# Joining the two layers of a two-layer attention network: layer 1's weights, first image and first projections move beside layer 0's last image, and the fallback branch moves to the program's end

## The chip, the cores and the metric

The kernel runs on one core of a Trainium2 chip. The metric is the device time of one execution in microseconds. All arithmetic is in 32-bit floats, except the feed-forward's weights, which hold signs.

## The reference

The input x has 8 images of 384 channels and 32 x 32 positions. Layer 0 is group norm (32 groups), an attention of 8 heads of 48 channels with a bias that depends on the relative position (from a small MLP), an output projection and the residual:

```python
qkv = (tokens @ qkv_w + qkv_b).reshape(b, n, 3, NUM_HEADS, HEAD_DIM)
attn = jnp.einsum('bhnd,bhmd->bhnm', q * scale, k) + relative_bias
attn = jax.nn.softmax(attn, axis=-1)
x = x + (attn_times_v @ proj_w + proj_b)
```

Layer 1 works on the 1024 tokens of each image: layer norm, an attention of 6 heads of 64 channels whose q and k are normalised over the 64 channels of a head, the residual, layer norm again, and a feed-forward of two linear maps with binarised weights (sign of the weight less its group's mean), whose outputs are scaled by the largest absolute value of a group of images. The groups are five of one image each, so images 5, 6 and 7 have a feed-forward that is zero.

```python
q, k = _normalize(q), _normalize(k)          # (t - mean) / std over a head's 64 channels
t = t + softmax(q @ k.T * scale) @ v @ proj_w.T + proj_b
h = gelu(quantize(ln(t) @ sign(W1 - mean).T + b1))
t = t + quantize(h @ sign(W2 - mean).T + b2)
```

## The kernel before

Two functions follow each other, `_layer0` (L97) and `_layer1` (L892); layer 0's result goes through a tensor x1 in DRAM. Each layer has pools of its own in SBUF and four PSUM tiles of two banks. Each engine runs its instructions in the order of the program text, since both layers are traced under a manual schedule; only the range check between them is ordered by a scheduler. `_Later` (L64) holds work that is due a number of steps later; `later.step()` runs once per unit or projection, and so writes the order of the engines' queues by hand. A "unit" is a pair of heads, a half of the queries and a quarter of the keys.

Layer 0: per image 32 units. `scores` (L419) makes 16 matmul instructions into two PSUM tiles s, DVE adds the position bias into an e tile (L437), ACT takes the exponential (L441); `weigh` (L447) multiplies e by v two units later (`LAG`). No row maximum is subtracted. The row sums come out as a row of the product; when a pair of heads is done, `divide` (L474) sends them through DRAM to 128 partitions, POOL takes the power -1 (L486), and after some steps the inverses come back spread over the rows (L494) and POOL multiplies (L498). The image's output projection, `project_out` (L514), normally runs at unit 3 of the next image. The last image has no next: it multiplies the first three pairs, calls `later.finish()`, and then multiplies the last pair, `wl`, into the same three PSUM tiles (L526), adds the residual (L538) and stores x1 (L541).

Since no maximum is subtracted, all row sums are kept in `sums`, and a range check (L593 to L603) reduces them to one flag. Its maximum over the partitions is a custom instruction of POOL (L602). The program loads the flag into registers and branches over `_layer0_shifted`, a slower general layer 0 that redoes x1, before `_layer1` begins:

```python
    _layer0(tc, ins, x1, flag)
    out_of_range = tc.nc.values_load(flag[0:1, 0:1])
    with tc.If(out_of_range > 0):
        _layer0_shifted(tc, ins, x1)
    _layer1(tc, ins, x1, out)
```

The flag is zero for the given inputs.

Layer 1 begins with the loads of its weights `L1_attn_qkv_wT` (L922) and its first image `bx` (L917). `center` (L957) subtracts from the projection's weights their mean over the input channels (18 matmul instructions with a matrix of ones, named cm, a copy on ACT, subtractions on DVE at L973) and their mean over a head's channels (L977 to L979), so that the layer norm's and the head's means need no work later. `attention_inputs` (L1458) then makes the token sums (squares on ACT, `token_sums`, named ts, tr, td, tc), the six projections of q and k (pq, L1023), head sums (hs, L1052), and `normalise_qk` (L1060): the sums go to DRAM (hd), to 128 partitions (hc), POOL takes a power (L1073), the result goes to DRAM (hi), the factors of k come back as kc, and those of q, spread over the rows, as rq (L1087); DVE multiplies q by rq (L1094). Its two step numbers say after how many steps rq is fetched and after how many more it is used. Last come the projections of v (pv, L1104). `sign_weights` (L1121) loads the feed-forward's weights in five raw tiles each, DVE sums them (L1139), a matmul gives the means (L1143), ACT writes the signs (L1147); a table in the main loop gives the step of each. All intermediate tiles of 128 x 1024 come from one pool of 16, `work`.

Attention in layer 1 has 24 units per image; ACT reads the scores from PSUM and applies kc as its scale (L1179). In images 0 to 4 the feed-forward is mixed with the next image's projections; images 6 and 7 get theirs from `attention_inputs`, as image 0 does.

## Time and profile before

| | |
|---|---|
| median of three runs | 3165.62 us (3164.66 to 3168.25) |
| the profiled execution's own time | 3169.41 us |
| its span, first to last instruction | 3166.5 us |
| mean granted TensorE clock | 0.988 |
| PE, DVE, ACT, POOL busy | 97%, 55%, 44%, 14% |
| layer 0's last output products begin | 1442.04 us |
| SP's first DMA of layer 1 | 1478.50 us |
| first scores of layer 1 | 1569.16 us |

PE is the matmul engine, PEld its weight loads, DVE, ACT, POOL and SP the vector, scalar, GpSimd and sync engines. A line of the timeline has the start and length in us, the engine, the line of the program, the operation, what it writes and reads, how many instructions it groups, and in brackets how long the engine had been idle and what ended that; "<-issue" means that the profile shows nothing it waited for. A matmul of 32-bit floats in the text is two instructions in the profile.

### The profile page before, as it was taken

The page shows a single profiled execution, that of the slowest core. Times are in us where ns is not written, and L with a number is a line of the kernel's source. Part 1 is how long each engine was busy: PE and PEld are TensorE (multiplying, and loading weights), DVE is VectorE, ACT ScalarE, POOL GpSimd, SP SyncE. Part 2 cuts the span into 40 slices and gives each one's busy share as a digit, 9 for nine tenths or more (in the row PEclk, how much of TensorE's full clock was granted, in tenths as well). Part 3 has the DMA queues.
Part 4 walks back from the last instruction along what each step waited for, and adds up shares of the span by engine and source line. Part 5 has one row for each costly group of instructions (what it writes and reads, how often), then busy time and mean ns, then how long its engine had stood idle before and what let it go on. Part 6 is the DMA issues. An engine that isn't in the chain of part 4 may idle for free.

```text
span 3166.5 us, 46012 instructions
## 1 busy us (share of the span) xinstructions
PE 3057.7 (97%) x19066; PEld 1572.0 (50%) x19066; DVE 1744.7 (55%) x1748; ACT 1400.7 (44%) x1763; POOL 458.8 (14%) x302
## 2 busy tenths in 40 slices
PE   8799999999999999996899999999999999999999
PEld 3254645455555546432445645645645555634343
DVE  2554737373645647273464764754754854844545
ACT  2452616252543526162272462553553643643535
POOL 0110202111111102021200301301201201211110
PEclk9899999999999999998999999999999999999999
DMA  7302020211212020203310110100101101101011
GB/s 178 107 18 79 22 82 16 69 35 25 73 23 81 19 79 22 62 16 105 75 42 22 44 33 22 62 17 21 61 22 27 51 22 29 53 18 62 15 49 42
DMA packets 102768, 150.49 MB, mean 48 GB/s; under 512 B 62260, under 2 KB 65828, under 8 KB 101784
## 3 DMA queue, kind: packets, MB, share of 16 engines
q1 hardware_dynamic: 99688, 147.41, 16.5%
q8 instruction: 153, 2.51, 0.3%
q14 instruction: 63, 0.52, 0.1%
q10 hardware_dynamic: 2864, 0.05, 0.1%
HBM read 111.05 MB, written 27.32 MB: 44 GB/s over the span
## 4 chain that ended last, share of the span: by engine, by line
PE 42%; DVE 4%; DMA 3%; ACT 2%; issue 1%; POOL 1%; SPq 0%; DVEq 0%; ACTq 0%; POOLq 0%
PE s L1168 11%; PE o L1217 10%; PE y2p L1419 5%; PE pq L1023 5%; PE pp L1279 4%; PE y1p L1365 3%; PE pv L1104 3%; POOL hc L1073 1%; PE sum L1240 1%; DVE lun L1319 1%; DVE un L1314 1%; DVE un L1311 1%; DMA rb<-rd 1%; PE tsa L992 1%; PE hs L1052 0%
## 5 line engine op out<-in xcount | busy, mean ns | idle before, releaser
L441 ACT ACTIVATE e<-e 128x1024 f32<-128x1024 f32 x512 | 534.8, 1056 | 461.6 <-DVE e L437 445.6
L437 DVE TENSOR_TENSOR e<-s,grow 128x1024 f32<-128x1024 f32 x512 | 601.1, 1218 | 190.6 <-PE s L426 186.9
L426 PE MATMUL s<-qk 48*64 48x512 f32 x4096 | 613.8, 595 | 23.3 <-DVE e L437 20.3
L457 PE MATMUL o<-e,v 64*64 64x512 f32 x4096 | 608.5, 592 | 0.0
L1179 ACT ACTIVATE e<-s,kc 128x512 f32<-128x512 f32 x768 | 463.5, 691 | 213.3 <-PE s L1168 195.3
L1168 PE MATMUL s<-qk,qk 64*64 64x512 f32 x3072 | 400.6, 601 | 9.9 <-DVE v L1114 9.1
L1217 PE MATMUL o<-e,v 64*64 64x512 f32 x3072 | 391.6, 591 | 0.2 <-ACT e L1179 0.2
L426 PEld LDWEIGHTS s<-qk 48*64 48x64 f32 x4096 | 232.3, 133 | 259.4 <-issue 92.8
L457 PEld LDWEIGHTS o<-e,v 64*64 64x64 f32 x4096 | 249.3, 134 | 192.6 <-issue 96.2
L1194 DVE TENSOR_TENSOR t<-t,e 128x1024 f32<-128x1024 f32 x192 | 231.3, 1222 | 79.2 <-ACT e L1179 79.2
L1023 PE MATMUL pq<-bx,L_attn_qkv_wT 128*128 128x512 f32 x576 | 254.4, 596 | 2.3 <-DVE L_attn_qkv_wT L979 2.1
L372 PE MATMUL pq<-xn,wqk 128*128 128x512 f32 x576 | 251.0, 597 | 1.8 <-DVE xn L353 1.8
L1168 PEld LDWEIGHTS s<-qk,qk 64*64 64x64 f32 x3072 | 146.0, 134 | 211.5 <-issue 128.2
L486 POOL TENSOR_TENSOR inv<-sums,over 128x16 f32<-128x16 f32 x32 | 92.9, 2904 | 1033.1 <-DMA sums<-sd 927.1
L1217 PEld LDWEIGHTS o<-e,v 64*64 64x64 f32 x3072 | 138.8, 133 | 191.4 <-issue 164.6
L372 PEld LDWEIGHTS pq<-xn,wqk 128*128 128x128 f32 x576 | 109.4, 191 | 143.6 <-issue 142.9
L1023 PEld LDWEIGHTS pq<-bx,L_attn_qkv_wT 128*128 128x128 f32 x576 | 107.7, 190 | 145.7 <-issue 140.4
L1191 DVE TENSOR_TENSOR t<-e,e 128x1024 f32<-128x1024 f32 x96 | 114.1, 1224 | 84.1 <-ACT e L1179 84.1
L1352 DVE TENSOR_REDUCE parts<-y 128x1 f32<-128x1024 f32 x75 | 90.0, 1218 | 95.2 <-ACT y L1349 95.0
L1073 POOL TENSOR_TENSOR hc<-hc,rsqrt 128x32 f32<-128x32 f32 x24 | 135.3, 5639 | 2.0
L1039 ACT ACTIVATE qsq<-pq 128x1024 f32<-128x1024 f32 x48 | 49.1, 1024 | 192.5 <-DVE qk L1033 92.1
L1104 PE MATMUL pv<-L_attn_qkv_wT,bx 128*128 128x384 f32 x384 | 130.9, 497 | 1.9 <-DVE meanL_ffn_W1T L1144 1.9
(149 smaller groups left out, 2935.3 us busy)
## 6 DMA issues: line engine op xcount, KB each, us to landing
rb<-rd SPq DMA_DIRECT2D x112, 256.0 KB
wide<-table SPq DMA_DIRECT2D x128, 114.2 KB
xn<-in_x_dram SPq DMA_DIRECT2D x24, 512.0 KB
res<-in_x_dram SPq DMA_DIRECT2D x24, 512.0 KB
x<-res SPq DMA_DIRECT2D x24, 512.0 KB
bx<-x SPq DMA_DIRECT2D x8, 1536.0 KB
rq<-hi SPq DMA_DIRECT2D x48, 256.0 KB
out_dram<-bx SPq DMA_DIRECT2D x24, 512.0 KB
```

Source lines behind the costliest of these rows:

```text
L372: nc.tensor.matmul(pq[:, h], wqk[:, k, s, 2 * pair : 2 * pair + 2, :].rearrange("p h d -> p (h d)"), xn[:, k, ts(h, HALF)], start=(k == 0) ...
L426: nc.tensor.matmul(s[j][ts(c, QP), i], qk[pair][rows, 1, ts(4 * m2 + 2 * i + c, QP)], qk[pair][rows, 0, ts(h, HALF)], start=True, stop=True,)
L437: nc.vector.tensor_add(e.rearrange("p (i q) -> p i q", i=2), s[j], bass.AP(near.tensor, near.offset, [near.ap[0], [-QROWS * IW, 2], [1, HA ...
L441: nc.scalar.activation(e, e, AF.Exp)
L457: nc.tensor.matmul(po[ts(j, S0), r], v[keys, 2 * m2 + i, 2 * pair + j, :], es[j][keys, ts(i, HALF)], start=(m2 == 0 and i == 0), stop=(m2 ...
L1023: nc.tensor.matmul(pq[:, h], wqkv[:, k, s * C + pair * P : s * C + (pair + 1) * P], xt[:, k, ts(h, HALF)], start=(k == 0), stop=(k == KC - 1),
L1073: nc.gpsimd.tensor_tensor(c, c, rsqrt.to_broadcast(list(c.shape)), ALU.pow)
L1104: nc.tensor.matmul(pv[:, i, 0:C], xt[:, k].rearrange("c (p m) -> c m p", m=MT)[:, 2 * m2 + i], wqkv[:, k, 2 * C : 3 * C], start=(k == 0), ...
L1168: nc.tensor.matmul(s[j][ts(c, QP), i], qk[pair, 1][rows, ts(4 * m2 + 2 * i + c, QP)], qk[pair, 0][rows, ts(h, HALF)], start=True, stop=True,)
L1179: nc.scalar.activation(e[:, ts(i, HALF)], s[j][:, i], AF.Exp, scale=kc[:, pair, j, m : m + 1])
L1194: nc.vector.tensor_add(total[j], total[j], e)
L1217: nc.tensor.matmul(po[ts(j, D1), r], v[keys, 2 * m2 + i, at : at + D1], es[j][keys, ts(i, HALF)], start=(m2 == 0 and i == 0), stop=(m2 == ...
```

## The change

The branch with the general path goes to the end of the program: if the flag is set, `_layer0_shifted` and then a whole second `_layer1` run and overwrite the output. So layer 1 no longer waits for the flag, and the two layers are traced under one manual schedule. The range check's five DVE and one POOL instructions become five stages that run at steps 5, 7, 9, 11 and 13 of image 1 of layer 1, on tiles of `work`.

Both layers share one PSUM pool, the constants `rsqrt` and `ones`, one place for an image and one for the projection's weights (`_Shared`). Layer 0's q, k and v weights become two views of one tile. In layer 1 even images use the shared place, odd ones a place of their own; before, they alternated between two. `_Start` holds what was the head of layer 1 and is called from units 5 to 23 of layer 0's last image: weights, image, the two halves of centring with ACT's copies into two of layer 0's nine e tiles, the subtractions on POOL instead of DVE.

What layer 0 needs for its last projection (`wp`, `wl`, `oT`, `rb` and others) moves to a pool `kept` on the other side of SBUF that stays open. `project_out` is split: after the last unit come the products of three pairs and `later.finish()`; the residual loads go out when layer 1 has made its first pools; the products of the last pair, the sums and the stores run at step 1 of layer 1, which is after its token sums and its first projection. Layer 1's pools take the option `reuse_waits="tile"`; `wide` and a new pool `room` (for w1, w2, rb) open only after that step. The steps of the raw weights and of the head normalisation in `attention_inputs` change. The main loops are the same but for their indentation.

```diff
+class _Shared:
+    def __init__(self, tc, ctx):
+        nc = tc.nc
+        self.pool = ctx.enter_context(tc.tile_pool(name="s_pool", bufs=1))
+        self.ps = ctx.enter_context(tc.tile_pool(name="s_ps", bufs=4, space=PSUM))
+        self.rsqrt = self.pool.tile([P, 1], F32, tag="rsqrt", name="rsqrt")
+        nc.gpsimd.memset(self.rsqrt, -0.5)
+        self.ones = self.pool.tile([P, P], F32, tag="ones", name="ones")
+        nc.gpsimd.memset(self.ones, 1.0)
+    def mm2(self, name):
+        return self.ps.tile([P, NH, HALF], F32, tag="p", name=name)
+    def image(self, name):
+        return self.pool.tile([P, KC, N], F32, tag="x", name=name)
+    def weights(self, name):
+        return self.pool.tile([P, KC * 3 * C], F32, tag="w", name=name)
+class _Start:
+    def __init__(self, tc, ins, x1, shared):
+        self.nc, self.ins, self.x1, self.shared = tc.nc, ins, x1, shared
+    def load_weights(self):
+        self.wqkv = self.shared.weights("wqkv").rearrange("p (k c) -> p k c", k=KC)
+        self.nc.sync.dma_start(
+            self.wqkv, self.ins["L1_attn_qkv_wT"].rearrange("(k p) c -> p k c", p=P)
+        )
+    def load_image(self):
+        self.image = self.shared.image("bx0")
+        self.nc.sync.dma_start(self.image, self.x1[0].rearrange("(k p) n -> p k n", p=P))
+    def means(self, temp, at, n):
+        nc = self.nc
+        pm = self.shared.mm2(f"cm{at}")
+        for h in range(-(-n // HALF)):
+            w = min(HALF, n - h * HALF)
+            for k in range(KC):
+                cols = slice(at + h * HALF, at + h * HALF + w)
+                nc.tensor.matmul(
+                    pm[:, h, :w], self.shared.ones, self.wqkv[:, k, cols],
+                    start=(k == 0), stop=(k == KC - 1),
+                )
+        self.mean = temp(f"cmean{at}")
+        nc.scalar.activation(
+            self.mean[:, :n], pm.rearrange("p h q -> p (h q)")[:, :n], AF.Copy, scale=1.0 / C
+        )
+    def subtract(self, at, n):
+        for k in range(KC):
+            w = self.wqkv[:, k, at : at + n]
+            self.nc.gpsimd.tensor_sub(w, w, self.mean[:, :n])
+    def heads(self, k):
+        nc = self.nc
+        w = self.wqkv[:, k, 0 : 2 * C].rearrange("p (h d) -> p h d", d=D1)
+        hm = self.shared.pool.tile([P, 2 * H1], F32, tag="hm", name=f"hm{k}")
+        nc.vector.tensor_reduce(hm, w, AX.X, ALU.add)
+        nc.gpsimd.tensor_scalar(hm, hm, 1.0 / D1, 1.0, ALU.mult, ALU.mult)
+        nc.gpsimd.tensor_sub(w, w, hm.unsqueeze(2).to_broadcast([P, 2 * H1, D1]))
+    def stages(self, temp):
+        first, rest = (0, 2 * HALF), (2 * HALF, 3 * C - 2 * HALF)
+        return [
+            (5, self.load_weights),
+            (6, self.load_image),
+            (10, lambda: self.means(temp, *first)),
+            (11, lambda: self.subtract(*first)),
+            (12, lambda: self.means(temp, *rest)),
+            (14, lambda: self.subtract(*rest)),
+            (19, lambda: self.heads(0)),
+            (21, lambda: self.heads(1)),
+            (23, lambda: self.heads(2)),
+        ]
-def _layer0(tc, ins, x1, flag):
+def _layer0(tc, ins, x1, sums, shared, beside):
...
+    keep = ExitStack()
+    kept = keep.enter_context(tc.tile_pool(name="a_kept", bufs=1, side="right"))
...
-        wqk = const.tile([P, KC, 2, 2 * NF0, S0], F32, tag="wqk", name="wqk")
-        wv = const.tile([P, KC, C], F32, tag="wv", name="wv")
+        both = shared.weights("w0")
+        wqk = both[:, 0 : KC * 2 * C].rearrange(
+            "p (k s h d) -> p k s h d", k=KC, s=2, d=S0
+        )
+        wv = both[:, KC * 2 * C :].rearrange("p (k c) -> p k c", k=KC)
...
+        pps = {}
+        def products(b, m, pairs):
+            if (b, m) not in pps:
+                pps[b, m] = mm2(f"pp{b}_{m}")
+            for k in pairs:
+                for h in range(NH):
+                    nc.tensor.matmul(
+                        pps[b, m][:, h], (wp[:, k] if k < NF0 else wl)[:, ts(m, P)],
+                        oT[:, k, ts(h, HALF)],
+                        start=(k == 0), stop=(k == (NF0 if b == B - 1 else NF0 - 1)),
+                    )
+        def residuals(b, temp):
+            res = []
             for m in range(KC):
-                res.append(etile(f"res{b}_{m}"))
+                res.append(temp(f"res{b}_{m}"))
                 nc.sync.dma_start(res[m], x[b, ts(m, P)].rearrange("p h w -> p (h w)"))
-            def products(m, pairs):
-                if pps[m] is None:
-                    pps[m] = mm2(f"pp{b}_{m}")
-                for k in pairs:
-                    for h in range(NH):
-                        nc.tensor.matmul(
-                            pps[m][:, h], (wp[:, k] if k < NF0 else wl)[:, ts(m, P)],
-                            oT[:, k, ts(h, HALF)],
-                            start=(k == 0), stop=(k == (NF0 if apart else NF0 - 1)),
-                        )
-            if apart:
-                for m in range(KC):
-                    products(m, range(NF0))
-                later.finish()
+            return res
+        def project_out(b, res, pairs):
             for m in range(KC):
-                products(m, range(NF0, NP0) if apart else range(NF0))
+                products(b, m, pairs)
                 nc.vector.scalar_tensor_tensor(
-                    res[m], flat2(pps[m]), bp[:, m : m + 1], res[m], ALU.add, ALU.add
+                    res[m], flat2(pps[b, m]), bp[:, m : m + 1], res[m], ALU.add, ALU.add
                 )
                 nc.sync.dma_start(x1[b][ts(m, P), :], res[m])
...
+        with_last = beside(etile)
...
+                if b == B - 1:
+                    for at, work in with_last:
+                        if at == i:
+                            work()
                 later.step()
...
+        for m in range(KC):
+            products(B - 1, m, range(NF0))
+        later.finish()
+    def load_rest(temp):
+        rest.extend(residuals(B - 1, temp))
+    def finish():
+        project_out(B - 1, rest, range(NF0, NP0))
+        keep.close()
+    rest = []
+    return load_rest, finish
...
+def _range_check(tc, sums, flag, temp):
...
+    return [
+        over, under, lambda: nc.vector.tensor_mul(good[0], good[0], every), worst,
+        lambda: nc.vector.tensor_copy(flag, bad[1][:, 0:1]),
+    ]
...
-def _layer1(tc, ins, x1, out):
+def _layer1(tc, ins, x1, out, shared, start, before=None, check=None):
...
+            return ctx.enter_context(tc.tile_pool(name=name, bufs=bufs, reuse_waits="tile"))
...
+            if b % 2 == 0:
+                t = shared.image(f"bx{b}")
+            else:
+                t = xp.tile([P, KC, N], F32, tag="x", name=f"bx{b}")
...
-        wqkv = chunked("L1_attn_qkv_wT", 3 * C)
-        first = load(0)
+        if before is not None:
+            before[0](wtile)
+        wqkv, first = start.wqkv, start.image
...
+        def rest_of_pools():
+            nonlocal wide, room, w1, w2
+            if before is not None:
+                before[1]()
+            wide = pool("b_wide", 1)
+            room = pool("b_room", 1)
+            w1 = room.tile([P, KC, FF], F32R, tag="w1", name="w1")
+            w2 = room.tile([P, FC, C], F32R, tag="w2", name="w2")
...
-                        head(pair - 1, 2, 1)
+                        head(pair - 1, *((3, 3) if pair == 1 else (5, 4)))
...
-            center()
-                ("L1_ffn_W1T", w1, 1, (4, 4, 4, 5, 5), 6, (7, 7, 8, 8, 9)),
-                ("L1_ffn_W2T", w2, 4, (7, 7, 8, 8, 9), 10, (11, 13, 15, 17, 19)),
+            ("L1_ffn_W1T", lambda: w1, (KC, FF // NG), 2, (5, 5, 5, 6, 6), 8, (9, 9, 9, 10, 10)),
+            ("L1_ffn_W2T", lambda: w2, (FC, C // NG), 7, (10, 11, 12, 13, 14), 16, (17, 18, 19, 22, 23)),
...
+        later.after(1, rest_of_pools)
         qk, kc = attention_inputs(0, xt)
...
+            if b == 1 and check is not None:
+                for i, stage in enumerate(check(wtile)):
+                    later.after(2 * i + 5, stage)
...
-    _layer0(tc, ins, x1, flag)
+    sums = state.tile([P, B, NP0, 2 * N // P], F32, tag="sums", name="sums")
+    with ExitStack() as main, tc.manual_schedule():
+        shared = _Shared(tc, main)
+        start = _Start(tc, ins, x1, shared)
+        before = _layer0(tc, ins, x1, sums, shared, start.stages)
+        _layer1(
+            tc, ins, x1, out, shared, start, before,
+            lambda temp: _range_check(tc, sums, flag, lambda name: temp(name, (P, HALF))),
+        )
     out_of_range = tc.nc.values_load(flag[0:1, 0:1])
     with tc.If(out_of_range > 0):
         _layer0_shifted(tc, ins, x1)
-    _layer1(tc, ins, x1, out)
+        with ExitStack() as again, tc.manual_schedule():
+            shared = _Shared(tc, again)
+            start = _Start(tc, ins, x1, shared)
+            late = again.enter_context(tc.tile_pool(name="late", bufs=2))
+            for _, stage in start.stages(
+                lambda name: late.tile([P, N], F32, tag="t", name=name)
+            ):
+                stage()
+            _layer1(tc, ins, x1, out, shared, start)
```

## The prediction

> **What bounds the kernel now.** I read the page first (busy shares, then the forty slices), then a table of busy times by stage over the end of layer 0 and the start of layer 1, then the chain and the timeline there, and last the queue of SP.
>
> ```profile
> PE 3057.7 (97%) x19066; PEld 1572.0 (50%) x19066; DVE 1744.7 (55%) x1748; ACT 1400.7 (44%) x1763; POOL 458.8 (14%) x302
> PEclk9899999999999999998999999999999999999999
> ```
>
> PE is busy 97% of the span, no other engine over 55%: PE time is kernel time, and a change pays only where PE stands still or runs at a low granted clock. The nineteenth and twentieth slices (1425 to 1583 us) hold the one dip in mid-kernel. By stage (window, length, busy time of PE, PEld, DVE, ACT, POOL with instruction counts, granted clock, DMA):
>
> ```profile
> 1420.00:1440.00 20.00, 20.00 (x189) 7.56 (x182) 14.25 (x13) 13.15 (x14) 7.16 (x4) 1.00 0.12 28
> 1442.00:1478.00 36.00, 22.81 (x51) 9.60 (x48) 7.35 (x10) 0.58 (x1) 5.83 (x3) 0.88 0.32 105
> 1478.00:1502.00 24.00, 11.81 (x42) 4.45 (x42) 6.44 (x14) 5.90 (x7) 0.13 (x2) 0.75 0.49 165
> 1538.00:1569.00 31.00, 18.10 (x58) 15.69 (x58) 12.07 (x20) 5.78 (x6) 5.63 (x2) 0.83 0.40 85
> 1580.00:1660.00 80.00, 80.00 (x714) 36.39 (x706) 55.99 (x57) 61.25 (x99) 0.00 (x0) 1.00 0.14 41
> ```
>
> Before and after the join PE is full at clock 1.00; between 1442 and 1569 it idles in three stages and its clock falls to 0.75. The timeline names the waits (start, length, engine, line, operation):
>
> ```profile
> 1442.04 15.72 PE L526 MATMUL pp<-oT,wp 128*128 128x512 f32 x36
> 1456.34 0.38 POOL L602 PARTITION_ALL_REDUCE worst<-bad  x1 [6.45 <-issue]
> 1463.71 2.33 POOL L498 TENSOR_TENSOR oT<-oT,rb 128x1024 f32<-128x1024 f32 x1 [6.99 <-issue]
> 1466.10 7.06 PE L526 MATMUL pp<-oT,wl 128*128 128x512 f32 x12 [8.35 <-POOLq L1606]
> 1486.04 7.98 PE L966 MATMUL cm<-L_attn_qkv_wT,ones 128*128 128x512 f32 x18 [12.88 <-DMA L_attn_qkv_wT<-in_L_attn_qkv_wT_dram]
> 1502.06 16.41 PE L1023 MATMUL pq<-bx,L_attn_qkv_wT 128*128 128x512 f32 x36 [2.14 <-DVE L_attn_qkv_wT L979]
> 1566.77 0.59 PE L1143 MATMUL gmL_ffn_W2T<-mineL_ffn_W2T,ones 128*128 128x5 f32 x2 [12.60 <-DVE mineL_ffn_W2T L1139]
> 1569.16 7.77 PE L1168 MATMUL s<-qk,qk 64*64 64x512 f32 x48
> 1577.09 1.95 PE L1217 MATMUL o<-e,v 64*64 64x512 f32 x16 [0.16 <-ACT e L1179]
> ```
>
> To be seen: 8.35 us of PE waiting until POOL has divided the last pair (POOL was at the range check's all-reduce); 12.88 for layer 1's weights, which start only after the branch (the chain has nothing but SP until 1478.50, then 7.09 us of that DMA); the centring until 1502; and 12.60 for W2's column sums, queued in DVE behind a multiply that waits for its DMA. The last is also seen on SP:
>
> ```profile
> 1533.37 8.06 SPq L1134 DMA_DIRECT2D rawL_ffn_W2T<-in_L_ffn_W2T_dram  x5
> 1541.48 2.54 SPq L1087 DMA_DIRECT2D rq<-hi  x2
> ```
>
> W2's five loads hold SP for 8.06 us, and the row scales rq of pair 0 go out only behind them.
>
> **The change part by part.** T is the start of the last image's output products, 1442.04. Before, the first o of layer 1 begins at 1577.09, 135.05 us after T, and from there PE is full. So I sum what PE does in that stretch afterwards, at the durations of full-clock rows.
>
> *Moved into the last image: centring.* Twelve matmul instructions of 512 columns and six of 128. A pq of twelve takes 5.15 us in the rows (36 in 15.45), so 0.43 each: 5.15, and 0.11 for a quarter of the columns: 0.64. PE is at 20.00 of 20.00 there, so all 5.8 us are paid. Their effect on the units: the output products of image 6 stand in the same place, take three of four PSUM tiles, and cost 15.65 from first matmul to the next s (1326.15 to 1341.80) for 15.45 of work; so 0.2 for each of two insertions, 0.4. ACT's two mean copies (1.19) lie beside 3.4 us units in which ACT works 2.2. DVE's three sums of 0.87 fit the 1.08 it idles per unit. POOL's subtracts are three like its L498 (2.37), three small ones and three of 768 columns (about 1.8 each by the same row), some 13 us in 100 where it works 20; behind them are only the divide's inv and multiply of pairs 0 to 2, needed at T. If that cover went, T would slip by as much. Two of nine e tiles go to the means, for about three units; three go to the residuals at unit 3 at no visible cost. Weights and image (1.7 and 1.5 MB) are issued on SP at units 5 and 6, behind image 6's stores; the divide's small transfers behind them have a dozen units to spare, and images 0 to 6 load 1.5 MB in the same place.
>
> *Stretch after T.* Products of three pairs, 36: 15.45. Token sums of image 0: 4.70 less 0.77 of waiting in image 7's row, 3.9 (ACT's squares need 3 us and stand behind the three bias loads, 6.45 of issuing; T+0.7+6.45+3 is before T+15.45). PSUM: pp holds three tiles, so pq waits until ACT has copied the sums out, 0.8 by image 7's rows (end 2814.98, copy 2815.15 and 0.59). First pq 5.15. Products of the last pair 5.15, five more pq 25.75, two head sums 2.0, v 15.8 (48 instructions), W1's mean 0.3, third head sums 1.0: s begins at T+75.3. From s to the first o 5.7, as in image 1 (1802.07 to 1807.74). Together 81.0, with the centring 87.2. Gain 135.05 - 87.2 = 47.9.
>
> *What must be hidden for that.* (a) The last pair: rb is issued at 1451.78 and another such pair lands in 4 to 5 us; without the all-reduce POOL multiplies at about T+15 to T+17. PE asks at T+25.3: 8 us of cover. Residuals now queue on SP behind rb, not ahead of it. (b) W1: SP stands behind the three stores of x1, whose sums come at T+27 to T+32, then five loads; before they landed within about 10 us; the sums are due at T+52. (c) rq of pair 0: the steps are now (3,3), so SP issues it behind pair 1's hi, which waits for POOL's power. From the end of pair 1's head sums: 5.2 to POOL, 5.7 there, 8.1 to the landing (image 7: 2857.5 to 2865.6), 1.2 on DVE: 20.2, so T+73.3 against s at T+75.3. Covered by 2 us, the thinnest place. DVE waiting there holds only the last v copy. (d) W2 loads come behind rq now and its sums lie in units 0 to 3; its mean is at unit 5, so the 12.6 us wait has no successor on PE. Its raw tiles keep 5 of 16 work tiles until units 6 to 12; with e, t and f I count 13 in use, so no wait.
>
> *Other moves.* The new head steps also hold for images 6 and 7: before, DVE waited 12.11 for pair 1's scales in the v copies; now for pair 0's, which leave SP at nearly the same time. 0 for the two, between a gain of the 4.45 us stall that follows in image 7, twice, and a loss of as much. Range check in image 1: 2.7 us of DVE and 0.4 of POOL with 6.45 and 6.99 around it, in units where POOL is idle; 0, up to 7 if DVE's copy of the flag waits a whole swap and PE behind it. Memsets, pools, shared places: image b+1 alternated between two places before, too; 0.
>
> *The branch.* It is on the path before (inside the 135.05) and is now at the end. From DVE's last sum to SP's first instruction were 3.61 us (1474.47 to 1478.08), store included; the end of the span has 3.85 from the last sum (3162.65) with no branch. So between 0 and 3.6; I take 1.0, nearer 0, as the two gaps hardly differ.
> The Trainium skill (Runtime: NRT & Kernel Launch, section Instruction fetch mechanics) speaks against: a taken branch whose target is outside the two pages held makes a fetch stall, and the branch now skips two layers. By the rows the branch in mid-kernel, also over a whole layer, shows no more than the 3.61; a stall of that whole gap in place of my 1.0 would make the sum 3121.3.
>
> *Sum.* 47.9 - 1.0 = 46.9. The profiled execution took 3169.41 (span 3166.5 and 2.9 around it): 3122.5. It stands 3.8 over the median of 3165.62, from which: 3118.7; I say 3119. About 0.2% (6 us) is what a measurement can tell from no change.
>
> **The rivals.** *R1, the scales come late.* Thin cover (c). For: before, pair 0 took 29.3 from its head sums (1519.47) to DVE's multiply (1548.75), under W2's loads. Against: those loads now stand behind. That delay gives T+53+29.3+1.2 = T+83.5, 8.2 us late: 3127. *R2, the layers do not overlap:* layer 1's first tiles wait until layer 0's last use of their space. For: they lie where layer 0's pools were, and the diff changes how reuse waits. Against: most of these tiles are done with at T. Then token sums start after the last stores, T+36 with 10 us of ACT's loads and squares ahead, and pq at T+46; from pq to the first o PE needs 55.7 unstalled: T+101.7 + 6.2, gain 27, 1 back: 3140. *R3, slower: the granted clock.* Without the pause PE runs full for 3.1 ms; if the clock of what follows the join, some 1590 us, were lower by more than 46.9/1590 = 2.9%, the kernel would be slower; at 4% it is 3182. For: the clock is granted, not fixed. Against: it is 1.00 in every full window, 1400 us after the start as well as 20 us after the pause.
>
> **How the numbers follow.** Forecast 0.70, R1 0.13, R2 0.10, R3 0.05, no change for a reason I don't see 0.02. Its own range: 3113 (nothing at the branch, and half of the two stalls of 4.45 gone in images 6 and 7) to 3125 (3.6 at the branch, 3 of PSUM or slot waits). With R1: 3113 to 3132, leaving out R2, R3 and the tails. Faster 0.93, same 0.02, slower 0.05.
>
> **What would show it.** Right: PE full from 1300 to 1600 at clock 1.00 but for about 1 us before the first pq; the cm matmuls among the s of the last image; no wait for weights or W2's sums; first o near 1530; the all-reduce inside image 1; a tail of 4 to 8 us after the last sum. Wrong: s waiting for DVE's rq multiply (R1), PE empty after 1464 until x1's last store (R2), or longer units at a clock below 1.00 after 1530 (R3). A PE wait at cm or in image 1's units near the check would show covers I priced at nothing.

## The result, and the profile after

The changed kernel takes 3123.45 us (median of four, 3122.57 to 3127.35), the one before 3165.35 on the same chip: a ratio of 0.9868, with a 95% interval of 0.9851 to 0.9885. That is 42 us or 1.3% less, 4.5 us over the 3119 that was forecast and inside the range. The profiled execution took 3124.0 us, with a span of 3122.2.

Cut at the same events in both traces, the span of the change divides so (all in us of the two profiled executions):

| stretch | before | after | difference | priced |
|---|---|---|---|---|
| start to the v projection of layer 0's last image | 1299.04 | 1296.64 | -2.4 | 0 |
| from there to T, the last output products | 143.00 | 149.71 | +6.7 | +6.2 |
| T to the first o of layer 1 | 135.05 | 80.27 | -54.8 | -54.05 |
| first o to the first matmul of image 0's second feed-forward product (y2p) | 187.1 | 198.8 | +11.7 | 0 |
| first to last y2p | 963.1 | 964.4 | +1.3 | 0 |
| last y2p to DVE's last sum (images 6 and 7) | 435.35 | 424.65 | -10.7 | 0 |
| DVE's last sum to the end | 3.85 | 7.78 | +3.9 | +1.0 |
| sum | | | -44.3 | -46.85 |

The first and fifth rows differ by as much among the traces of kernels that are the same there (1293.9 to 1299.5, and 961.6 to 964.7). Three rows need a cause that the forecast did not have: +11.7, -10.7 and +3.9.

The page of the kernel after: busy time of the engines, and PE's busy share and granted clock in forty slices:

```profile
PE 3049.8 (98%) x19066; PEld 1579.0 (51%) x19066; DVE 1736.5 (56%) x1735; ACT 1400.7 (45%) x1762; POOL 472.9 (15%) x314
...
PE   8799999999999999999899999999999999999998
...
PEclk9899999999999999999999999999999999999999
```

The clock's dip in mid-span is gone from the forty slices, but PE's twentieth slice (1483 to 1561 us) shows an 8 among nines. A table of busy times by stage (window, length, busy time of PE, PEld, DVE, ACT, POOL, granted clock, DMA) finds a hole in it:

```profile
1440.00:1460.00 20.00, 20.00 (x91) 9.31 (x81) 3.23 (x6) 6.64 (x7) 3.98 (x3) 1.00 0.21 34
1460.00:1480.00 20.00, 19.29 (x63) 7.82 (x62) 5.08 (x4) 1.61 (x2) 4.97 (x7) 1.00 0.51 184
1520.00:1540.00 20.00, 19.98 (x172) 9.66 (x172) 15.63 (x16) 14.47 (x25) 5.70 (x2) 1.00 0.54 109
1540.00:1560.00 20.00, 11.21 (x84) 3.50 (x86) 8.58 (x11) 7.85 (x12) 0.00 (x0) 0.83 0.34 106
```

PE is full where it stood still before, and stands still in 1540 to 1560, early in layer 1's units, where it was full. The timeline of PE in the kernel after, from the moved centring to that hole (start, length, engine, line, operation, how many; in brackets the idle time before and its releaser):

```profile
1363.62 5.42 PE L146 MATMUL cm<-wqkv,ones 128*128 128x512 f32 x12
...
1375.99 0.94 PE L146 MATMUL cm<-wqkv,ones 128*128 128x128 f32 x6
...
1446.35 15.72 PE L608 MATMUL pp<-oT,wp 128*128 128x512 f32 x36
...
1465.48 5.42 PE L1128 MATMUL pq<-bx,wqkv 128*128 128x512 f32 x12 [0.71 <-ACT tra L1102]
1470.74 5.31 PE L608 MATMUL pp<-oT,wl 128*128 128x512 f32 x12
...
1520.94 6.04 PE L1272 MATMUL s<-qk,qk 64*64 64x512 f32 x45
1526.62 0.64 PE L1321 MATMUL o<-e,v 64*64 64x512 f32 x1
...
1551.34 3.49 PE L1321 MATMUL o<-e,v 64*64 64x512 f32 x16 [8.79 <-DVE oT L1331]
```

The join runs as forecast: the last pair's products start at 1470.74 without a wait, 0.71 us is lost before the first pq, the first o comes 80.27 after T. The hole begins 16 us later: an o waits 8.79 us for a PSUM tile that DVE has yet to copy out at L1331. The next 16 matmul instructions then take 3.49 us where the same ones take 1.9 at full clock. Why DVE is late is in its own queue:

```profile
1537.99 1.21 DVE L1199 TENSOR_TENSOR qk<-qk,rq 128x1024 f32<-128x1024 f32 x1
1546.99 1.23 DVE L1199 TENSOR_TENSOR qk<-qk,rq 128x1024 f32<-128x1024 f32 x1 [7.79 <-DMA rq<-hi]
1548.32 2.36 DVE L1295 TENSOR_TENSOR t<-e,e 128x1024 f32<-128x1024 f32 x2
1550.60 0.68 DVE L1331 TENSOR_TENSOR oT<-o,oT 128x512 f32<-128x512 f32 x1
```

The second L1199 is the multiply of pair 2's q, whose product is first read at unit 16; its step puts it into unit 4. It waits 7.79 us for its scales, and behind it stand two sums and the copy that PE waits for. And the scales are late because of SP (the queue of DMA issues; length is the time that issuing took):

```profile
1514.44 8.41 SPq L1237 DMA_DIRECT2D rawL_ffn_W2T<-in_L_ffn_W2T_dram  x5
1522.95 2.43 SPq L1192 DMA_DIRECT2D rq<-hi  x2
1525.48 0.59 SPq L1163 DMA_DIRECT2D hd<-hr  x1
1530.32 0.34 SPq L1176 DMA_DIRECT2D hc<-hd  x1
...
1540.66 2.08 SPq L1192 DMA_DIRECT2D rq<-hi  x2
```

W2's loads, which were taken out of the way of pair 0, now hold SP in front of pair 2's hd and its whole chain of hc, power, hi and rq. In the trace before, the same multiply waits 1.60 us at 1588.09 and PE does not notice.

So the candidates to be tested: (A) the +11.7 is pair 2's multiply in DVE's queue, with W2's loads as what makes it late; (B) the -10.7 comes from the new steps of pairs 0 and 1, which hold for images 6 and 7 too; (C) the +3.9 is the branch at the end. Rivals: that the gain at the join is the branch's going and not the order of the queues; that the way pools are reused plays a part; and that the loss after the first o belongs to contention, not to a queue.

### The profile page after: what moved, and what is told of

It is laid out like the page before. It is cut to its first block, busy times and chain, and to the rows that moved or that the text cites. A ratio compares the mean times of both kernels' runs of the same rounds, so it can differ in the third digit from the quotient of the medians.

```text
span 3122.2 us, 45962 instructions
## 1 busy us (share of the span) xinstructions
PE 3049.8 (98%) x19066; PEld 1579.0 (51%) x19066; DVE 1736.5 (56%) x1735; ACT 1400.7 (45%) x1762; POOL 472.9 (15%) x314
## 4 chain that ended last, share of the span: by engine, by line
PE 84%; DVE 4%; DMA 3%; ACT 2%; POOL 1%; issue 1%; SPq 1%; DVEq 0%; ACTq 0%; POOLq 0%
PE s L513 14%; PE o L544 14%; PE s L1272 10%; PE o L1321 10%; PE pq L459 7%; PE y2p L1523 5%; PE pp L608 4%; PE y1p L1469 4%; PE pq L1128 4%; PE pp L1383 4%; PE pv L487 4%; PE pv L1209 3%; POOL hc L1178 1%; PE sum L1344 1%; DMA rb<-rd 1%
## 5 line engine op out<-in xcount | busy, mean ns | idle before, releaser
L1272 PE MATMUL s<-qk,qk 64*64 64x512 f32 x3072 | 394.2, 592 | 2.2 <-DVE v L1219 1.9
L544 PEld LDWEIGHTS o<-e,v 64*64 64x64 f32 x4096 | 255.1, 133 | 185.9 <-issue 82.4
L1128 PE MATMUL pq<-bx,wqkv 128*128 128x512 f32 x576 | 254.1, 596 | 0.7 <-ACT tra L1102 0.7
L459 PE MATMUL pq<-xn,w 128*128 128x512 f32 x576 | 251.0, 597 | 1.8 <-DVE xn L440 1.8
L1321 PEld LDWEIGHTS o<-e,v 64*64 64x64 f32 x3072 | 140.1, 133 | 199.8 <-issue 161.0
L459 PEld LDWEIGHTS pq<-xn,w 128*128 128x128 f32 x576 | 109.4, 191 | 143.4 <-issue 143.4
L1128 PEld LDWEIGHTS pq<-bx,wqkv 128*128 128x128 f32 x576 | 107.8, 190 | 143.5 <-issue 141.4
L1209 PE MATMUL pv<-wqkv,bx 128*128 128x384 f32 x384 | 131.1, 497 | 0.0
```

Source lines behind the costliest of these rows:

```text
L459: nc.tensor.matmul(pq[:, h], wqk[:, k, s, 2 * pair : 2 * pair + 2, :].rearrange("p h d -> p (h d)"), xn[:, k, ts(h, HALF)], start=(k == 0) ...
L544: nc.tensor.matmul(po[ts(j, S0), r], v[keys, 2 * m2 + i, 2 * pair + j, :], es[j][keys, ts(i, HALF)], start=(m2 == 0 and i == 0), stop=(m2 ...
L1128: nc.tensor.matmul(pq[:, h], wqkv[:, k, s * C + pair * P : s * C + (pair + 1) * P], xt[:, k, ts(h, HALF)], start=(k == 0), stop=(k == KC - 1),
L1209: nc.tensor.matmul(pv[:, i, 0:C], xt[:, k].rearrange("c (p m) -> c m p", m=MT)[:, 2 * m2 + i], wqkv[:, k, 2 * C : 3 * C], start=(k == 0), ...
L1272: nc.tensor.matmul(s[j][ts(c, QP), i], qk[pair, 1][rows, ts(4 * m2 + 2 * i + c, QP)], qk[pair, 0][rows, ts(h, HALF)], start=True, stop=True,)
L1321: nc.tensor.matmul(po[ts(j, D1), r], v[keys, 2 * m2 + i, at : at + D1], es[j][keys, ts(i, HALF)], start=(m2 == 0 and i == 0), stop=(m2 == ...
```

## The experiments

Times are medians, each against the kernel before on the same chip, so ratios are compared across groups; the kernel after has 0.9868. The kernel before took 3165.14 beside the runs with pair 2's multiply later, the old steps of pairs 0 and 1, no branch after the change, and centring at the join. It took 3164.11 beside those with the weights' old steps, the early flag, the kernel before without its branch, and pools without the option, and 3168.05 beside the other three.

**Pair 2's multiply used later.**

```diff
-            head(NP1 - 1, 3, 2)
+            head(NP1 - 1, 3, 9)
```

> The changed kernel (3123.5) with one number changed: in the inputs of images 0, 6 and 7 the multiply of pair 2's q by its scales stands 9 steps after their fetch in DVE's queue, not 2. Theory: PE's 8.8 us wait at unit 5 of image 0 is DVE waiting at that multiply for a late transfer, with o's copy queued behind it; the wait and the slow clock after it (11.7 us against the same stretch of the kernel before) go: 3112, between 3110 and 3116. Rival: DVE is late there because of W2's column sums among the units, or o waits for a work tile; then the wait stays wherever the multiply is: 3121 to 3125.

Measured: 3113.22 us (3111.39 to 3117.17), ratio 0.9836 (0.9820 to 0.9853). DVE and PE of this kernel, timeline:

```profile
1540.62 0.68 DVE L1331 TENSOR_TENSOR oT<-o,oT 128x512 f32<-128x512 f32 x1
...
1565.22 1.22 DVE L1199 TENSOR_TENSOR qk<-qk,rq 128x1024 f32<-128x1024 f32 x1
```

```profile
1538.59 2.85 PE L1272 MATMUL s<-qk,qk 64*64 64x512 f32 x16
1541.36 1.95 PE L1321 MATMUL o<-e,v 64*64 64x512 f32 x16
```

The copy runs at 1540.62, the o follows without a wait and at full speed, and the multiply, 25 us later, waits for nothing. First o to first y2p falls from 198.8 to 188.4: 8.8 of waiting and 1.6 of low clock. W2's loads are where they were (8.13 us on SP at 1513.45), and pair 2's rq goes out as late as in the kernel after (95.3 us after T for 94.3), so it was not their lateness alone that PE paid for, nor contention with the loads. With the next two this is the fastest kernel of the study, 10 us under the change and 52 under the kernel before.

**Two units later only.**

```diff
-            head(NP1 - 1, 3, 2)
+            head(NP1 - 1, 3, 4)
```

> The changed kernel with pair 2's multiply 4 steps after its fetch instead of 2 (9 took the whole wait away, 3113.2). Theory: DVE meets the multiply two units, 6.9 us, later, when the scales are about 1 us away: PE's wait falls from 8.8 to below 2, 3112 to 3116. Rival: nine steps helped for another reason, the place of the multiply behind the end of the first half's sums; then 4 steps keep most of the wait: 3118 to 3124.

Measured: 3116.61 us (3116.42 to 3118.44), ratio 0.9838 (0.9822 to 0.9855). DVE's wait shrinks from 7.79 to almost nothing, and it lies where a sum, not PE's copy, stands behind:

```profile
1544.03 0.68 DVE L1331 TENSOR_TENSOR oT<-o,oT 128x512 f32<-128x512 f32 x1
...
1548.93 1.23 DVE L1199 TENSOR_TENSOR qk<-qk,rq 128x1024 f32<-128x1024 f32 x1 [0.25 <-DMA rq<-hi]
```

PE no longer waits at the o. Two of the twelve units of slack are enough.

**W2's loads behind pair 2, the multiply left alone.**

```diff
-("L1_ffn_W2T", lambda: w2, (FC, C // NG), 7, (10, 11, 12, 13, 14), 16, (17, 18, 19, 22, 23)),
+("L1_ffn_W2T", lambda: w2, (FC, C // NG), 14, (18, 19, 20, 21, 22), 24, (25, 26, 27, 28, 29)),
```

> The changed kernel (3123.5) with W2's loads, sums, mean and signs seven and more steps later, so that they stand behind pair 2's scales on SP; pair 2's multiply stays 2 steps after its fetch. Theory: the scales are late because W2's loads hold SP and the DMA engines in front of them (sums out 3.8 us late, their way through DRAM 3.0 longer, rq as in the changed kernel); they arrive about 7 us earlier and of PE's 8.8 us wait at most 2.5 stay: 3112 to 3117. Rival: the chain itself (sums, 5.4 us of power on POOL, the spread) is too long for the two steps whatever SP does: wait 5 or more, 3118 to 3124.

Measured: 3115.56 us (3114.69 to 3116.39), ratio 0.9836 (0.9819 to 0.9852). SP, then DVE:

```profile
1536.76 1.22 SPq L1192 DMA_DIRECT2D rq<-hi  x2
1538.08 9.59 SPq L1237 DMA_DIRECT2D rawL_ffn_W2T<-in_L_ffn_W2T_dram  x5
```

```profile
1542.00 1.23 DVE L1199 TENSOR_TENSOR qk<-qk,rq 128x1024 f32<-128x1024 f32 x1 [1.85 <-DMA rq<-hi]
```

With the loads behind, the multiply at its old place waits 1.85 us, about what it did before the change (1.60), and PE has no wait at o. Pair 2's head sums end 74.7 us after T in both kernels; hd goes out at 75.4 here and at 79.1 in the kernel after, and its way to hc takes 1.8 us here and 4.8 there. So of the 6.8 us by which the chain is late 3.8 are SP's queue, and 3.1 a slower trip behind the transfers in front of it. The loss needs both: the loads in front of pair 2's chain and the multiply 12 units ahead of its use. Taking away either gives the 10 us back, by the ratios; in this trace 9.1 of it lies between the first o and the first y2p, and 2.0 in a shorter tail (see the flag loaded early).

**The weights' old steps.**

```diff
-("L1_ffn_W1T", lambda: w1, (KC, FF // NG), 2, (5, 5, 5, 6, 6), 8, (9, 9, 9, 10, 10)),
-("L1_ffn_W2T", lambda: w2, (FC, C // NG), 7, (10, 11, 12, 13, 14), 16, (17, 18, 19, 22, 23)),
+("L1_ffn_W1T", lambda: w1, (KC, FF // NG), 1, (4, 4, 4, 5, 5), 6, (7, 7, 8, 8, 9)),
+("L1_ffn_W2T", lambda: w2, (FC, C // NG), 4, (7, 7, 8, 8, 9), 10, (11, 13, 15, 17, 19)),
```

> The changed kernel with the old steps for the loads, sums, means and signs of W1 and W2. Theory: W2's loads hold SP in front of the scales of pair 0 again and W2's mean stands in PE's queue before the scores, so part of the old 12.6 us wait returns: 3130 to 3140. Rival: with the rest of the change the old steps do as well, and pair 2's transfers come earlier, which shortens the 8.8 us wait: 3115 to 3124.

Measured: 3121.07 us (3120.33 to 3124.82), ratio 0.9867 (0.9851 to 0.9884). The expectation of a slower kernel missed. PE's timeline shows why:

```profile
1503.48 17.57 PE L1209 MATMUL pv<-wqkv,bx 128*128 128x384 f32 x48 [1.87 <-DVE meanL_ffn_W1T L1247]
...
1526.99 8.21 PE L1272 MATMUL s<-qk,qk 64*64 64x512 f32 x48 [4.82 <-DVE qk L1199]
1535.36 1.95 PE L1321 MATMUL o<-e,v 64*64 64x512 f32 x16 [0.16 <-ACT e L1283]
```

T to the first o takes 91.7 us in place of 80.3, as the theory had it, since W2's loads stand in front of pair 1's sums and pair 0's scales; but first o to first y2p takes 187.0 in place of 198.8. The rival was right in the time, and wrong in that pair 2's scales come earlier: its head sums end 3.9 us later here, and its rq goes out 94.3 us after T in both kernels (1537.91 here). The units begin 11 us later, and so DVE comes to pair 2's multiply when its scales are there. The change of these steps moved one delay from before the first o to behind it; alone it is worth nothing. The 10 us come only when pair 2's multiply is moved as well.

**The old steps of pairs 0 and 1.**

```diff
-                        head(pair - 1, *((3, 3) if pair == 1 else (5, 4)))
+                        head(pair - 1, 2, 1)
```

> The changed kernel with the old steps (2,1) for the scales of pairs 0 and 1, in images 0, 6 and 7. Theory: the 10.7 us that the last three images gained come from these steps, so 7 to 10 us return there; and in image 0 DVE waits for pair 1's scales behind W2's loads, some 5 to 10 us more, part of which is taken from the later 8.8 us wait: 3130 to 3142, and the waits of s for the v copies in images 6 and 7 are 4 to 5 us each again. Rival: the gain in images 6 and 7 comes from something else (shared places, the order of image loads); then these images stay as they are and the time is 3123 to 3130.

Measured: 3136.21 us (3133.49 to 3139.32), ratio 0.9906 (0.9890 to 0.9923), 12.8 over the change. Where the scores of image 6 begin, first in the kernel before, then in the one after, then in this one, each from its timeline:

```profile
2876.51 6.64 PE L1168 MATMUL s<-qk,qk 64*64 64x512 f32 x32 [4.45 <-DVE v L1114]
```

```profile
2825.14 1.22 DVE L1199 TENSOR_TENSOR qk<-qk,rq 128x1024 f32<-128x1024 f32 x1 [3.86 <-DMA rq<-hi]
...
2826.77 2.18 DVE L1219 TENSOR_SCALAR v<-pv,tca 128x384 f32<-128x384 f32 x4
...
2835.58 3.66 PE L1272 MATMUL s<-qk,qk 64*64 64x512 f32 x32 [1.07 <-DVE v L1219]
```

```profile
2829.45 1.23 DVE L1199 TENSOR_TENSOR qk<-qk,rq 128x1024 f32<-128x1024 f32 x1 [13.16 <-DMA rq<-hi]
2830.59 1.14 DVE L1219 TENSOR_SCALAR v<-pv,tca 128x384 f32<-128x384 f32 x2
...
2840.30 5.36 PE L1272 MATMUL s<-qk,qk 64*64 64x512 f32 x32 [4.40 <-DVE v L1219]
```

With the old steps DVE waits 13.16 us for scales in front of the v copies, and PE's scores wait 4.40 for the PSUM tiles that these copies free; the 32 matmul instructions after that take 5.36 us for 3.66. With the new steps DVE copies two v tiles, waits 3.86, and PE loses 1.07. This happens in image 6 and in image 7: last y2p to last sum is 438.2 here and 424.7 in the kernel after, 13.5 us. (B) holds. At image 0 the old steps cost 11 before the first o (91.4 us for 80.3) and give back 9.8 behind it (189.0 for 198.8): again the same delay, in another place.

**No branch and no general path after the change.** The output for other inputs would lack the general path.

```diff
-    out_of_range = tc.nc.values_load(flag[0:1, 0:1])
-    with tc.If(out_of_range > 0):
-        _layer0_shifted(tc, ins, x1)
-        with ExitStack() as again, tc.manual_schedule():
...
-            _layer1(tc, ins, x1, out, shared, start)
```

> The changed kernel without the load of the flag, the branch and the general path behind it (the fallback for row sums out of range is left out; the check itself still runs). Theory: the 7.8 us from the last sum to the end, against 3.85 before, are the branch: 3119.5, and the tail is 3.9 again. Rival: the tail is the landing of the last stores or the wind-up of a longer program: 3123.5, tail 7.8.

Measured: 3116.35 us (3114.75 to 3119.31), ratio 0.9846 (0.9829 to 0.9862). The last DVE sum of the kernel after and of this one, from their timelines:

```profile
3113.14 1.28 DVE L1388 SCALAR_TENSOR_TENSOR bx<-pp,L_attn_proj_b,bx 128x1024 f32<-128x1024 f32 x1 [0.43 <-PE pp L1383]
```

```profile
3109.75 1.28 DVE L1388 SCALAR_TENSOR_TENSOR bx<-pp,L_attn_proj_b,bx 128x1024 f32<-128x1024 f32 x1 [0.43 <-PE pp L1383]
```

The first ends at 3114.42 in a span of 3122.2, the second at 3111.03 in one of 3114.7: tails of 7.78 and 3.67. The branch with its path costs 4.1 us at the end. (C) holds. The rest of the difference lies, by the two traces, between the first o and the first y2p (0.6 us; the wait at the o is 7.4 here for 8.8), between first and last y2p (1.8) and in images 6 and 7 (1.3), which differ as much between other kernels that are the same there.

**The flag loaded early.** The registers are filled before image 2's units, more than 1 ms before the branch.

```diff
-    out_of_range = tc.nc.values_load(flag[0:1, 0:1])
+    out_of_range = regs[0]
```

> The changed kernel with the flag loaded into registers before the units of image 2, and only the comparison and the branch at the end. Theory: the load of the flag is about half of the 3.9 us that the tail has grown: 3121.5, tail near 6. Rival: it is the jump over two layers: 3123.5 and a tail of 7.8.

Measured: 3121.71 us (3118.66 to 3124.32), ratio 0.9868 (0.9851 to 0.9884). The tail is 7.9 us, as with the load at the end. The load is not what costs; my theory falls, and what follows the load holds the 4.1 us. The traces show where. SP's waits behind the last sum, in the kernel after, then in the one without the branch (what waits, for what, us in total, times, longest), and instruction packets in the same stretch of the kernel after (packets, MB, share of the DMA engines):

```profile
SPq L1721 <- SPq L1721: 4.9, 2, 2.8
```

```profile
SPq L1759 <- DMA out_dram<-bx: 2.2, 1, 2.2
```

```profile
q14 instruction: 5, 0.04, 1.6%
```

L1721 is the branch. SP's test and jump take 0.05 us; then two gaps of 2.8 and 2.0 us stand in front of SP's next instructions, with nothing outside SP that they wait for. Without the branch SP waits 2.2 us for the last store to land, and no instruction packet comes in behind the last sum. With it five come in, 8 KB each, and each gap ends shortly (0.4 and 1.1 us) after one has landed. From the last sum to the end of the first gap are 3.9 us; without the branch SP goes on 2.7 us after the sum: 1.2 of the 4.1 us. The second gap holds 2.1, and some more semaphore instructions behind it the other 0.8. With the flag early SP jumps 0.6 us sooner after the last sum, and the first gap ends 4.0 us after it all the same. In two kernels with the branch, W2's loads behind pair 2 and centring at the join, four packets come in, the second gap is missing, and the tail is 5.8 us; in the other eight it is 7.6 to 8.0. So the jump is what costs. That the gaps are waits for these packets is read from the times; the trace doesn't name it.

**The kernel before without its branch.** Here too only the general path is left out.

```diff
-    out_of_range = tc.nc.values_load(flag[0:1, 0:1])
-    with tc.If(out_of_range > 0):
-        _layer0_shifted(tc, ins, x1)
```

> The kernel before (3165.3) without the load of the flag, the branch and the general path (the fallback is left out; the check's own instructions remain). Theory: the branch was worth no more than the 3.6 us between the last sum and SP's first load, since the order of the queues keeps the rest: 3160 to 3163. Rival: the branch was the wall, and without it layer 1's loads and means slide under layer 0's last products by themselves: 3145 or less.

Measured: 3160.56 us (ten runs, 3158.04 to 3165.46) against 3164.11, ratio 0.9989 (0.9980 to 0.9999): 3.5 us, with an interval from 0.3 to 6.3. PE's waits at the join are all there; its timeline:

```profile
1465.71 7.35 PE L526 MATMUL pp<-oT,wl 128*128 128x512 f32 x12 [10.30 <-POOL oT L498]
1483.17 7.81 PE L966 MATMUL cm<-L_attn_qkv_wT,ones 128*128 128x512 f32 x18 [10.11 <-DMA L_attn_qkv_wT<-in_L_attn_qkv_wT_dram]
...
1561.95 0.59 PE L1143 MATMUL gmL_ffn_W2T<-mineL_ffn_W2T,ones 128*128 128x5 f32 x2 [10.49 <-DVE mineL_ffn_W2T L1139]
```

SP issues the first load of layer 1 directly behind the last store of x1, at 1474.91, and T to the first o is still 133.0 us. So what the change gained at the join it gained by the order of the queues; the branch was some 2 to 3.5 of it, about as much as it now costs at the end.

**Weights, image and centring at the join.** They are called behind the last steps of layer 0, not at units 5 to 23 of its last image.

```diff
-                if b == B - 1:
-                    for at, work in with_last:
-                        if at == i:
-                            work()
...
         later.finish()
+        for _, work in with_last:
+            work()
```

> The changed kernel with the loads of layer 1's weights and image and their centring moved back, out of the last image's units to behind its last products (same instructions, subtractions still on POOL). Theory: half of the gain is that these stand beside the units: weights land some 8 us after the products, then 5.8 of means, 1.2 of copy, 7 of subtraction and the heads' means stand in front of the first projection: about 20 us more, 3143 (3138 to 3150). Rival: the gain is the branch and its barrier alone, and the chain would be hidden beside the last products: 3123 to 3128.

Measured: 3137.88 us (3135.10 to 3139.63), ratio 0.9910 (0.9893 to 0.9926). PE's timeline:

```profile
1458.12 7.08 PE L146 MATMUL cm<-wqkv,ones 128*128 128x512 f32 x12 [3.89 <-DMA wqkv<-in_L_attn_qkv_wT_dram]
...
1476.54 8.32 PE L1126 MATMUL pq<-bx,wqkv 128*128 128x512 f32 x12 [3.30 <-POOL wqkv L166]
```

T comes 6.7 earlier by the centring's own time, and T to the first o grows from 80.3 to 102.1 by that work and the waits for it: 15.1 us net in the traces, where the medians differ by 14.4. I had expected 5 more, since I forgot that the 6.7 come back to the units. Beside the last image the weights cost PE their own 6.4 us and no wait.

**The range check at the join again.** Its five stages run in front of layer 0's last steps, not in image 1.

```diff
+        for stage in _range_check(tc, sums, flag, lambda name: etile(name, (P, HALF))):
+            stage()
         later.finish()
```

> The changed kernel with the range check back at the join, on POOL in front of the last pair's multiply, as it ran in the kernel before. Theory: the all-reduce with 6.5 us before and 7 us after it moves the multiply from 1461.4 to about 1470, and PE, which now has token sums and a projection to do, asks for it at 1470.7: covered but for 2 us at most, 3122 to 3127. Rival: moving the check was itself what removed the 8.35 us wait; then PE waits 4 to 8 us at the last pair's products, 3127 to 3133.

Measured: 3128.43 us (3125.67 to 3131.51), ratio 0.9878 (0.9861 to 0.9894). POOL, then PE:

```profile
1459.87 0.38 POOL L716 PARTITION_ALL_REDUCE worst<-bad  x1 [6.09 <-DMA rb<-rd]
1468.77 2.34 POOL L585 TENSOR_TENSOR oT<-oT,rb 128x1024 f32<-128x1024 f32 x1 [8.53 <-DMA tca<-tda]
```

```profile
1471.16 5.42 PE L608 MATMUL pp<-oT,wl 128*128 128x512 f32 x12 [1.29 <-POOL tiny L1078]
```

The last pair's multiply slips by 7.4 us against the kernel after (1461.38 there), 8.4 counted from T, and PE waits 1.29 (tiny is the small POOL instruction directly behind the multiply). In the kernel after, the multiply ends 17.4 us after T and PE asks for it at 24.4; these 7.0 us of cover take up nearly all of the slip, and by the ratio (0.0010 of 3168, 3 us, with intervals that overlap) little is left. So with the new order of the products the check's place hardly matters. That the order did more than the check's place isn't shown: with the check away and the old order PE would ask at 15.7, by the same rows, and wait some 1.7 us, an estimate that no run tests. Each of the two moves by itself would take away most of the 8.35 us.

**Pools without the option.**

```diff
-            return ctx.enter_context(tc.tile_pool(name=name, bufs=bufs, reuse_waits="tile"))
+            return ctx.enter_context(tc.tile_pool(name=name, bufs=bufs))
```

> The changed kernel with layer 1's pools at the default for reused space instead of the option for single tiles. Theory: what layer 1 needs early lies over space that is done with when the last products start, so the option changes nothing: 3123.5, between 3121 and 3126. Rival (R2 of the prediction): with the default the first tiles wait until all of layer 0's pools are done, and PE stands behind ACT's loads and squares: 3127 to 3140.

Measured: 3125.81 us (3121.31 to 3126.18), ratio 0.9878 (0.9862 to 0.9895). T to the first o takes 80.3 us here as well. The option bears on no wait that PE sees.

## Why the prediction was right, and where its steps were not

The time was inside the range and the stated mechanism carried it: PE full across the join, first o 80.27 us after T (81.0 summed). But the sum of 46.9 came out close to the spans' 44.3 because two terms that it priced at nothing, +11.7 and -10.7, cancel. That is luck. Point by point:

- *Centring in the last image, 5.8 + 0.4*: 5.42 + 0.94 = 6.36 us of PE, and the stretch grew by 6.7. Right; ACT, DVE and POOL took their parts without holding PE.
- *The stretch after T, 81.0*: right, and so are its covers. (a) POOL multiplied the last pair at T+15.0 and PE did not wait, with 7.0 us of cover for the 8 stated; (b) W1's sums came with no wait; the first pq lost 0.71 for the 0.8 stated.
- *(c), the thinnest place*: pair 0's multiply ended at T+73.2 and the scores began at T+74.6, for T+73.3 and T+75.3. R1's place was the right one to watch, and held, by 1.4 us.
- *(d) "W2 loads come behind rq now ... so no wait"*: this is the step that failed. It followed the loads away from pair 0's scales and W2's sums and mean into the units, and did not ask which small transfers now stand behind the loads on SP. They are pair 2's (its hd 3.8 us late on SP, and 3.1 more on the way to hc), and its multiply, whose step was not edited and which therefore was not priced, held DVE for 7.79 us and PE for 8.79, plus 1.6 of low clock: 10.4 of the 11.7 by the run that moves it. Moving the multiply, or moving the loads, each undoes it.
- *Images 6 and 7, "0 for the two"*: measured -10.7. The reading that DVE would wait for pair 0's scales at nearly the same time missed that two of the v copies now stand ahead of that wait and that the wait itself shrinks from about 13 to 3.86 us. The bound, twice 4.45, covered the waiting (4.45 and 4.63 before, 1.07 and 0.87 after: 7.1 us less) but left out the low clock behind each wait (6.64 us before and 3.66 after, for the same 32 matmul instructions). The rows that the prediction calls image 7's, 2815 to 2866, are image 6's in the program's count.
- *The branch, 1.0 between 0 and 3.6*: 4.1 by the run without it, over the upper bound. That two gaps, 3.61 in mid-kernel with the branch and 3.85 at the end without, "hardly differ" was no evidence: one runs from a sum to SP's next instruction, the other to the end of the last store, so they need not hold the same parts. Taken from the kernel before, the branch was worth 3.5 (0.3 to 6.3).
- *The Trainium skill's rule against the change* (Runtime: NRT & Kernel Launch, section Instruction fetch mechanics: a taken branch to a target outside the pages held stalls the fetch) pointed the right way; the page gives no figure. The runs give 4.1 us that an early load of the flag leaves untouched, a test of 0.05 us, and behind it SP's gaps with instruction packets coming in. This agrees with a stalled fetch, as far as times alone can tell.
- *The range check in image 1, 0 up to 7*: nothing. PE is busy 20.00 of 20.00 in every window from 1740 to 1840, around the all-reduce at 1803.78.
- *R2 and R3*: pq began 19 us after T with no wait for stores, and none for space but the 0.71 us for ACT's copy that was priced; the option on the pools changes nothing; the granted clock is 1.00 in the full windows after the join, and first to last y2p is 1.3 us longer, not 2.9%. Both fall.
- *The profiled execution against the median*: of the 4.5 us over the forecast, 3.3 are this. The execution before stood 3.8 over its median, the one after 0.55; the correction was that of a single execution.

What stays open: the remaining 1.3 us behind the first o, which the version with the later multiply keeps as well; why four instruction packets come in at the end of two kernels and five in the others; and how the 54.8 us at the join divide among all the moves, since only some were taken back one by one.

## What to carry to other kernels

When a transfer is moved, list every instruction that then stands behind it in its queue, those with unchanged steps too, and follow each to the in-order engine that consumes it: a multiply scheduled 12 units ahead of its use cost nothing until its data came 8 us later, and then stopped everything behind it. Place such a consumer near its use, not near its producer; here one number (2 to 9) was worth 10 us. And look past the end of the stretch that is summed before a gain is booked: what was saved ahead of the first o was in part lost 16 us behind it.

## What the runs showed of the hardware that was not expected

- A branch over the general path costs 4.1 us at the program's end (tails of 7.78 and 3.67 us; 5.8 in two kernels with the branch) and 3.5 in mid-kernel (3164.11 to 3160.56, interval 0.3 to 6.3), and loading its flag more than 1 ms ahead saves none of it (tail 7.9). Its test takes 0.05 us; the time lies behind the jump, where instruction packets of 8 KB come in.
- The clock's price depends on the length of the wait: after 8.79 us of waiting 16 matmul instructions took 3.49 us for 1.95, after 4.40 us 32 took 5.36 for 3.66, after 3.89 us (centring at the join) 12 took 7.08 for 5.42, and after 1.07 us 32 took 3.66. A wait of 3.9 us or more cost 1.5 to 3.0 us more than itself (the last by the 6.64 us of the kernel before, after 4.45), one of about 1 us nothing. The Trainium skill (TensorE: Matmul & The Clock Gate, Part 1, on the clock gate) has the rule behind it: half the clock after an idle window of about 3.4 us, and a busy window as long until it is whole again. The rows agree in which waits cost and which don't. By the page's figure one such window at half clock would lose about 1.7 us, an estimate; the rows of 1.5 to 1.7 fit it, the 3.0 is more.
- POOL's all-reduce stood with 6.09 us of idle time before it and 8.53 behind it at the join, between ordinary tensor operations. In image 1, where the operation before it on POOL was the feed-forward's own all-reduce, it came 36.88 us after that one, took 1.37 us, and held nobody. Why the idle time stood around it at the join, no run here shows.
